# Second attention of a two-layer network on one core: where the value products stand in a step, where the layer matrices are made, and when the last slots are told

## The chip, the core and the metric

The kernel runs on one core of one Trainium2 chip. The core has five engines that the text names as the profile does: PE (matrix products and transposes; PEld are the weight loads that go with them), DVE (vector), ACT (scalar functions and copies), POOL (vector work and indirect DMAs) and SP (DMA issue). They run their own instruction streams and wait for each other on semaphores. Products land in PSUM, which has 8 banks of 128 x 512 float32 numbers. The metric is the device time of one launch in microseconds, as the median of several runs.

## What is computed

The input is 32 sequences of 128 tokens with 128 features, `x`, and one condition vector for each sequence. The network has two layers, each a chain of a conditioned map, an attention, a second conditioned map and a feed-forward part. Everything is in float32. The change lies in the second layer, which is, cut to what matters:

```python
# experts: a gate picks 2 of 4 experts for each sequence, plus a shared one
y = sum_e w[e] * (gelu(x @ ew1[e] + eb1[e]) @ ew2[e] + eb2[e]) + gelu(x @ sw1 + sb1) @ sw2 + sb2
# attention, 16 heads of 8
Q, K, V = relu(y @ Wq + bq), relu(y @ Wk + bk), relu(y @ Wv + bv)
scores = mask(Qh @ Kh.T / sqrt(8))            # key mask and causal mask
out = softmax(scores) * query_mask @ Vh + y
y = gamma * (out - mean) / sqrt(var + 1e-8) + beta
# a low-rank conditioned map: y = y + y @ M, with M of each sequence from its condition
# slots: 64 slots a sequence
alpha = softmax over the 8 largest of ((gelu([y, slot_mean] @ w1 + b1) @ w2 + b2) / tau)
si = (alpha.T @ y) / alpha.sum                # what each slot takes in
S_new = gru(si, slots)                        # r, z, n gates
T = softmax(q(S_new) @ k(S_new).T * scale) @ v(S_new) + S_new
out = alpha @ (layernorm(T) @ wvp + bvp) @ wo + bo
```

The output of the kernel is the stream with that last `out` added.

## The kernel before

**Tiling.** The stream X lies in SBUF with the features on the partitions; a chunk is 4 sequences, 512 columns, and there are 8 chunks. The first layer runs before the part that matters here. The second layer runs in a loop at the end (from L1479) of rounds `i`, in turns of TURN = 32 rounds, one turn for each of NP = 4 pairs of chunks, and two turns of rounds more for what trails. In a turn, with `r = i // 32` and `k = i % 32`:

- k = 0 to 23 are the **expert phase** of pair r: each round runs one `ins` and one `outs` piece (`shared_in`, `chosen_in`, `shared_out`, `chosen_out`, L860 to 913). A `chosen_in` multiplies X with an expert's fetched weights `ew` and ACT makes `he` (gelu) of it; a `chosen_out` multiplies `he` with `ew`.
- k = 23 and 24 to 31 each call `advance` with one of the pair's 8 sequences, and k = 0 to 2 of the next turn call it without one, to drain: the **attention**. In the last pair nothing of experts follows: that is the **tail**.

**An attention step.** `advance` (L1412) is a software pipeline written out by hand. Each call starts one sequence (masks and scores), works on the one before it (`w1`: highest, weights, early), on the one two before (`t1`: turned, kept, early_weights), three before (`v1`: values, valued), four before (`b1`: back, sums, normed) and five before (`n1`: moments). The functions are at L959 to 1072:

- `masks(hg)` and `scores()`: products into one PSUM bank for each of four head groups. 12 blocks of 128 rows of scores come of a sequence: `s_0` to 7 for the late queries and 8 to 11 for the early ones.
- `highest(hg)`: DVE takes maxima (`s1m`), each second one combines them (`s1max`); `weights(hg)`: ACT makes two exponentials (`s<-ps,s1max`); `early(hg)`: DVE subtracts the maxima for the early block and so frees the bank; `early_weights`: one exponential for all four (`s<-s`).
- `turned(c)`: PE transposes four blocks; `kept(c)`: ACT copies them to SBUF (`p1T`); `values`: 32 products with V; `valued`: ACT copies the sum (`oS`); `back`: PE transposes it; `sums`, `normed`: DVE divides (`rsum`, `o`), POOL adds to R.

PSUM banks have tags: scores take five banks A and B, all else three banks C in rotation (`ps()`, L294). In a step the order of takers is turned 1, turned 0, back, values, turned 2, so `values` takes the bank that `kept` 1 frees.

**What sets the order.** A scheduler orders the instructions of an engine by itself, except those that are pinned: ACT's activations always run in program order (`act`, L378), and so do DVE's and PE's while `pinned` isn't empty (L244 to 261), which `advance` sees to for its whole body. The rest is placed by a timetable: `plan` and `at` (L1339, L1391 to 1409) say in which round a generator starts, and `steps(i)` (L1465) moves each running generator one `yield` further a round. In attention rounds `steps` is called inside `advance`, as the last of `last`.

**The generators that the change touches.**

- `attention_inputs` (L915): V, the query mask, then q and k (a product, an activation, a product, an activation), then the mask sum (`tt` of 0.69 us), R, then the copies of V. For the first chunk of a pair it is in the timetable at k = 13; for the second one it is called by `next(inputs)` in k = 24 to 26.
- `after_attention` (L1110): moments, the root by ten small DVE instructions (`root_of`), `nmr`; then ACT normalizes R; transposes, X; products with the layer matrices, `xc`; transposes back, `xn`. For the second chunk it also starts `hs`.
- `layer_made` (L1095): a product on POOL (`rb`), four on PE, two additions on DVE: the two layer matrices `lw` of a pair. They lie in buffers `h1`, which the outputs `ot` of `slots_told` use too; `rb` lies in buffer `h3`, which the V of `attention_inputs` uses too.
- `hidden`, `routes_top`, `routes_exp`, `routes` (L1146 to 1207): gelu, logits and their 8 largest, two exponentials (`lg`), weights `al` and what the slots take in. `slots_new`, `slots_exp`: the gates and the slots' own scores.
- `slots_told` (L1266): the slots' softmax on DVE; transposes and copies (`sl_pT`, `y`); products with the values; moments and a root on DVE (`rsy`); transposes and copies (`ot`, `yT`); two more rounds of products and additions; a transfer of `ot` to the output. Five to six rounds long.

For pairs 0, 1 and 3 `slots_told` starts in rounds 5 and 7 of the turn after the slots' exponentials (L1407 to 1409), for pair 2 in rounds 26 and 27 of the turn itself, in the middle of pair 3's attention.

Of the kernel before, what the change touches and what calls it, by code (L numbers as in the profile page):

```python
# [19 lines left out]
P = 128  # L20
# [221 lines left out]
def program(ctx, tc, out, xT, packs, where):  # L242
# [37 lines left out]
    def w(name):  # L280
        pack, rows, c0, n = where[name]
        return loaded[pack][:rows, c0 : c0 + n]
# [21 lines left out]
    def mm(out_, lhsT, rhs, start=True, stop=True):  # L304
        T.matmul(out_, lhsT=lhsT, rhs=rhs, start=start, stop=stop)
# [72 lines left out]
    def act(*args, **kwargs):  # L378

        return tc.keep_in_program_order(A.activation(*args, **kwargs))  # L380
# [534 lines left out]
    def attention_inputs(g):  # L915
        xm = XMs[g]

        vf = mpool.tile([P, CB, D], F32, tag="h3", name="vf", bufs=1)
        qm = pool.tile([P, CB], F32, tag="qm", name="qm", bufs=2)
        for k in range(2):  # L920
            p = ps()
            p3 = p[:, : 2 * (D + 1)].rearrange("p (b d) -> p b d", d=D + 1)
            for e in range(2):
                mm(p3[:, e], xm[:, bass.ts(2 * k + e, S)], w("wv"))
            tt(V, vf[:, 2 * k : 2 * k + 2], p3[:, :, 0:D], outer(w("bv"), 2), ALU.add)
            V.tensor_scalar(qm[:, 2 * k : 2 * k + 2], p3[:, :, D], 0.0, None, ALU.not_equal)

        mask16 = pool.tile([P, CB, S], BF16, tag="mask16", name="mask16", bufs=2)
        G.tensor_scalar(mask16, inner(qm, S), -1.0, 1.0, ALU.mult, ALU.add)
        p = ps()  # L930
        mm(p, w("wq"), xm)
        qT = pool.tile([P, CH], F32, tag="qT", name="qT", bufs=2)
        act(qT, p, AF.Relu, bias=w("bq"))
        p = ps()
        mm(p, w("wk"), xm)
        kT = pool.tile([P, CH], F32, tag="kT", name="kT", bufs=2)
        act(kT, p, AF.Relu, bias=w("bk"))
        MVs[g] = pool.tile([P, CB, 2], F32, tag="mv", name="mv", bufs=2)
        prep[g] = qT, kT, mask16, qm
        yield  # L940

        p = ps()
        for b in range(CB):
            mm(p[:, bass.ts(b, S)], mask16[:, b, :], bars16)
        tt(V, mask16, b3(p), outer(causal, CB), ALU.add)
        yield

        p = ps()
        for b in range(CB):
            T.transpose(p[:, bass.ts(b, S)], xm[:, bass.ts(b, S)], ident)  # L950
        R = Rs[g] = pool.tile([P, CB, D], F32, tag="R", name="R", bufs=2)
        act(R, b3(p), AF.Copy)
        yield
        v, vo = V1[g % 2]
        for b in range(CB):
            act(v[:, 2 * b : 2 * b + 2, :, 0:8], vf[:, b].rearrange("p (h t d) -> p t h d", t=2, d=8), AF.Relu)
        nc.sync.dma_start(vo[64:P], v.rearrange("p (b t) h d -> p b t h d", t=2)[0:64, :, 1])
# [152 lines left out]
    def after_attention(g):  # L1110

        R, mv = Rs[g], MVs[g]
        for b in range(CB):
            moments(g, b)
        rs = root_of(mv[:, :, 1], "rs", 1e-8)
        nm = pool.tile([P, CB], F32, tag="nmr", name="nmr", bufs=2)
        V.scalar_tensor_tensor(nm, mv[:, :, 0], -1.0, rs, ALU.mult, ALU.mult)
        yield
        for b in range(CB):
            act(R[:, b, :], R[:, b, :], AF.Identity, scale=rs[:, b : b + 1], bias=nm[:, b : b + 1])  # L1120
        yield
        p = ps()
        for b in range(CB):
            T.transpose(p[:, bass.ts(b, S)], R[:, b, :], ident)
        V.scalar_tensor_tensor(col(g), p, w("gamma"), col(g), ALU.mult, ALU.add)
        yield
        p = ps()
        for b in range(CB):
            mm(p[:, bass.ts(b, S)], LWs[g][:, b, :], col(g)[:, bass.ts(b, S)])
        xc = XCs[g] = mpool.tile([P, CH], F32, tag="F", name="xc", bufs=3)  # L1130
        tt(V, xc, col(g), p, ALU.add)
        yield

        if g % 2:
            HSs[g // 2] = ps()
            for k in range(2):
                mm(HSs[g // 2][NS * k : NS * k + NS], w("f_w1a"), XCs[g - 1 + k])

        xn = XNs[g] = pool.tile([P, CB, D + 1], F32, tag="xn", name="xn", bufs=2)
        G.memset(xn[:, :, D : D + 1], 1.0)  # L1140
        p = ps()
        for b in range(CB):
            T.transpose(p[:, bass.ts(b, S)], xc[:, bass.ts(b, S)], ident)
        act(xn[:, :, 0:D], b3(p), AF.Copy)
# [121 lines left out]
    def slots_told(g):  # L1266
        s, m, sv = TKs[g]
        sn = SNs[g]
        V.tensor_reduce(m, s, AX.X, ALU.add)
        V.reciprocal(m, m)  # L1270
        tt(V, s, s, inner(m, NS), ALU.mult)
        yield
        p = ps()
        for q in range(2):
# [111 lines left out]
    for r in range(NP):  # L1386
        a, c = 2 * r, 2 * r + 1
        t = TURN * r
        if r:
            at(t + 13, attention_inputs, a)  # L1390
        at(t + 24, beta_added, a)  # L1391
        at(t + 24, beta_added, c)
        t += TURN
        at(t + 0, after_attention, a)
        at(t + 0, layer_made, r)
        at(t + 3, after_attention, c)
        at(t + 7, hidden, r)
        at(t + 8, routes_top, a)
        at(t + 9, routes_top, c)
        at(t + 12, routes_exp, r)  # L1400
        at(t + 13, routes, a)
        at(t + 14, routes, c)
        at(t + 17, slots_new, a)
        at(t + 18, slots_new, c)
        at(t + 25, slots_exp, r)

        t += 26 if r == NP - 2 else TURN + 5  # L1407
        at(t, slots_told, a)
        at(t + (1 if r == NP - 2 else 2), slots_told, c)
    line = []  # L1410

    def advance(item=None, between=()):  # L1412

        line.append(item)
        w1, t1, v1, b1, n1 = (line[-k] if k <= len(line) else None for k in (2, 3, 4, 5, 6))

        def do(it, name, *args):
            if it:  # L1420
                it[name](*args)

        first, last = between or ((), ())
        pinned.append(True)
        do(item, "masks", 0)
        do(w1, "highest", 0)
        do(w1, "highest", 1)
        if w1 or t1:
            do(v1, "kept", 2)
        do(t1, "turned", 1)  # L1430
        do(w1, "weights", 0)
        do(t1, "kept", 1)
        do(t1, "turned", 0)
        do(w1, "weights", 1)
        for f in first:
            f()
        do(w1, "highest", 2)
        do(w1, "highest", 3)
        do(b1, "back")
        do(w1, "weights", 2)  # L1440
        do(v1, "values")
        do(w1, "early", 0)
        do(n1, "moments")
        do(t1, "kept", 0)
        do(w1, "early", 1)
        do(b1, "sums")
        do(w1, "early", 2)
        do(w1, "weights", 3)
        for hg in range(1, 4):
            do(item, "masks", hg)  # L1450
        do(item, "scores")
        do(t1, "early_weights")
        do(b1, "normed")
        do(v1, "valued")
        for f in last:
            f()
        do(t1, "turned", 2)
        do(w1, "early", 3)
        if not item:
            do(w1, "early_weights")  # L1460
        if not w1:
            do(t1, "kept", 2)
        pinned.pop()
# [10 lines left out]
    for i in range(END + 2 * TURN):  # L1474
        r, k = i // TURN, i % TURN
        if i < 24:
            if i == 0:
                first_pieces()
            if i == 23:  # L1479
                advance(attention(0, 0))  # L1480
            continue
        if r < NP and k == 0:
            ins, outs, _ = (p + q for p, q in zip(experts(2 * r), experts(2 * r + 1)))
            ins[0]()
        if k < 3 and 1 <= r <= NP:
            advance()
        if k >= 24 and r < NP:
            b = k - 23
            if k == 24:
                inputs = attention_inputs(2 * r + 1)  # L1490
            between = [], [lambda: steps(i)]
            if k < 27:
                between[k > 25].append(lambda: next(inputs, None))
            if k == 25:
                between[1].append(lambda: next(inputs))
            advance(attention(2 * r + b // CB, b % CB) if b < 2 * CB else None, between)
            continue
        if r < NP:
            if k:
                ins[k]()  # L1500
            if k == 23:

                act(cst[0:1, 0:1], zeros[0:1, 0:1], AF.Exp)
            outs[k]()
            if k == 23:
                advance(attention(2 * r, 0))
        steps(i)
# [30 lines left out]
```

## Time and profile before

| what | us |
|---|---|
| median of 3 runs (lowest, highest) | 1293.98 (1291.41, 1294.65) |
| the profiled execution | 1292.62 |
| its span | 1290.8 |
| first layer and what is mixed with it, up to 748 | 748 |
| attention of turn 0, 1, 2, 3, first to last exponential | 63.0, 43.0, 43.1, 52.4 |
| expert phases, three, from first to last piece | 77 to 82 each |
| tail behind the last attention | 91.8 |

The mean granted clock of PE is 0.934. PE is busy 1122.5 us (87% of the span), PEld 716.1, DVE 752.3, ACT 741.9 and POOL 489.0. In a row of busy times by stretch, each engine has its microseconds and, in brackets, its instructions; then come the granted clock (1.00 is full), the share of the DMA engines and GB/s. In the chain of waits each line is a start, a length, an engine and what it worked on; the line that follows is what waited for it. In the timeline of an engine each line is a start, a length and the operation; a bracket at its end tells how long the engine was idle before it and who released it.

### The profile page before, as it was taken

What the parts mean: (1) busy time and instruction counts of PE and PEld (TensorE: products, weight loads), DVE (VectorE), ACT (ScalarE), POOL (GpSimd) and SP (SyncE); (2) the same over time, 40 slices, a digit from 0 to 9 for tenths busy, and PEclk for the clock granted to TensorE, in tenths of its full rate; (3) what the DMA queues carried; (4) which work ended last, traced back from release to release, by engine and by line L of the source; (5) the groups of instructions that cost most, each with busy time, mean ns of one, the idle gap of its engine ahead of it and who ended that gap; (6) DMA issues with size and microseconds to landing.
All of it is one profiled execution on the core that took longest, in us unless ns stands there. A gap on an engine that the chain in (4) does not pass through costs nothing. (4 is left out here: it accounts for less than half of the span.)

```text
span 1290.8 us, 24290 instructions
## 1 busy us (share of the span) xinstructions
PE 1122.5 (87%) x9509; PEld 716.1 (55%) x9509; DVE 752.3 (58%) x1996; ACT 741.9 (57%) x1857; POOL 489.0 (38%) x433
## 2 busy tenths in 40 slices
PE   4999899989999899898988677998999899987655
PEld 1555555445554455455545446676677667766433
DVE  1344748465684655836545467556755675568443
ACT  2666565665646646545355555676965596567421
POOL 1565555546555455534354531133222321312000
PEclk9999999989999989889898887999999999999765
DMA  6000000000000000000242210143024302400000
GB/s 258 1 1 2 1 1 1 1 1 1 1 2 1 1 1 1 1 1 1 93 129 64 81 36 6 56 146 104 11 77 136 109 10 76 134 21 11 18 0 17
DMA packets 18322, 51.99 MB, mean 40 GB/s; under 512 B 1568, under 2 KB 7840, under 8 KB 17952
## 3 DMA queue, kind: packets, MB, share of 16 engines
q0 software_dynamic: 9648, 40.01, 10.0%
q1 hardware_dynamic: 7984, 9.38, 2.3%
q8 instruction: 75, 1.23, 0.4%
q10 hardware_dynamic: 576, 1.05, 0.2%
q14 instruction: 39, 0.32, 0.1%
HBM read 46.25 MB, written 2.10 MB: 37 GB/s over the span
## 5 line engine op out<-in xcount | busy, mean ns | idle before, releaser
L380 ACT ACTIVATE s_sb<-ps,s_max 128x128 f32<-128x128 f32 x512 | 139.2, 383 | 132.6 <-DVE s_max L256 126.3
L256 POOL TENSOR_TENSOR s_sb<-s_sb,s_sum 128x1024 f32<-128x1024 f32 (+1 forms) x64 | 119.7, 1871 | 76.7 <-DVE s_sum L256 58.0
L256 PE MATMUL ps<-hT,w_attn 128*128 128x512 f32 x256 | 125.0, 618 | 10.9 <-DVE hT L256 10.9
L256 POOL TENSOR_TENSOR s_half<-s_sb 128x512 f32<-128x512 f32 x62 | 79.5, 1282 | 110.6 <-ACT s_sb L380 110.5
L256 POOL DMA_INDIRECT ew<-in_expert,rows x64 | 63.2, 987 | 124.4 <-DVE ye L256 98.2
L380 ACT ACTIVATE qk<-ps 128x512 f32<-128x512 f32 x128 | 74.4, 615 | 62.1 <-PE ps L256 61.6
L256 DVE TENSOR_REDUCE s_max<-ps 128x4 f32<-128x512 f32 x128 | 81.2, 674 | 49.0 <-PE ps L256 48.7
L380 ACT ACT_TABLE_LOAD x61 | 78.3, 1283 | 52.4 <-DVE s_max L256 38.9
L380 ACT ACTIVATE s<-ps,s1max 128x128 f32<-128x128 f32 x256 | 79.3, 400 | 39.5 <-DVE s1max L256 31.6
L256 DVE TENSOR_REDUCE s_sum<-s_half 128x8 f32<-128x256 f32 x62 | 25.8, 416 | 121.3 <-POOL s_half L256 121.2
L256 PEld LDWEIGHTS ps<-qk 64*128 64x128 f32 x1024 | 68.0, 195 | 37.4 <-issue 37.4
L256 PEld LDWEIGHTS ps<-hT,w_attn 128*128 128x128 f32 x256 | 47.5, 195 | 70.3 <-issue 48.4
L256 PE MATMUL ps<-he,ew 128*128 128x128 f32 x512 | 77.6, 291 | 5.8 <-ACT he L380 4.9
L380 ACT ACTIVATE he<-ps,ew 128x128 f32<-128x128 f32 x256 | 70.7, 377 | 20.2 <-issue 10.7
L256 PE MATMUL ps<-qk 64*128 64x128 f32 x1024 | 81.6, 294 | 0.0
L256 PEld LDWEIGHTS ps<-he,ew 128*128 128x128 f32 x512 | 67.8, 195 | 22.3 <-ACT he L380 11.6
L256 PE MATMUL ps<-w_base,s_sb 128*128 128x128 f32 x512 | 75.1, 291 | 3.6 <-ACT s_sb L380 2.7
L256 PE MATMUL ps<-pT,v 128*64 128x128 f32 x1024 | 73.2, 287 | 4.7 <-DVE X L256 2.5
L256 PE MATMUL ps<-X,ew 128*128 128x128 f32 x512 | 73.6, 278 | 0.7 <-DMA ew<-in_expert,rows 0.7
L256 DVE TENSOR_REDUCE s1m<-ps 128x6 f32<-128x384 f32 x128 | 65.0, 548 | 14.3 <-PE ps L256 14.3
L256 PEld LDWEIGHTS ps<-X,ew 128*128 128x128 f32 x512 | 65.6, 192 | 7.8 <-issue 6.1
L256 PEld LDWEIGHTS ps<-pT,v 128*64 128x64 f32 x1024 | 57.5, 142 | 17.5 <-issue 7.1
(298 smaller groups left out, 2429.4 us busy)
## 6 DMA issues: line engine op xcount, KB each, us to landing
v1o<-v SPq DMA_DIRECT2D x8, 256.0 KB, 3.0
out_x<-ot SPq DMA_DIRECT2D x8, 256.0 KB, 2.3
X<-in_xT ACTq DMA_DIRECT2D x4, 256.0 KB, 7.2
X<-in_xT SPq DMA_DIRECT2D x4, 256.0 KB, 9.8
w_attn<-in_attn POOLq DMA_DIRECT2D x1, 1024.0 KB
w_lowr<-in_lowr SPq DMA_DIRECT2D x1, 1024.0 KB
ew<-in_expert,rows POOLq DMA_INDIRECT x64, 5.3
w_ffn<-in_ffn SPq DMA_DIRECT2D x1, 928.0 KB, 10.4
```

Of the source, the lines that this page charges most:

```text
L256: ins = f(*args, **kwargs)
L380: return tc.keep_in_program_order(A.activation(*args, **kwargs))
```

## The change

- In `advance` the order of a step is new: the exponentials of two head groups come ahead of the copies of `kept` 2, those of the others ahead of `kept` 1 and `kept` 0; the last two maxima come ahead of what `first` holds; `values` stands behind the scores.
- `attention_inputs` yields between the products and the activations of q and k, so it has one round more, and the calls for the second chunk move accordingly.
- The moments and the root of `after_attention` and the softmax of `slots_told` are pinned to their places in program order.
- `layer_made` of pairs 1 to 3 starts in round 19 of the pair's expert phase and not at the start of the next turn.
- `slots_told` of pair 2 starts, as that of the others, in rounds 5 and 7 of the turn after, which is the tail.

```diff
--- before.py
+++ after.py
@@ -930,11 +930,12 @@
         p = ps()
         mm(p, w("wq"), xm)
         qT = pool.tile([P, CH], F32, tag="qT", name="qT", bufs=2)
+        pk = ps()
+        mm(pk, w("wk"), xm)
+        kT = pool.tile([P, CH], F32, tag="kT", name="kT", bufs=2)
+        yield
         act(qT, p, AF.Relu, bias=w("bq"))
-        p = ps()
-        mm(p, w("wk"), xm)
-        kT = pool.tile([P, CH], F32, tag="kT", name="kT", bufs=2)
-        act(kT, p, AF.Relu, bias=w("bk"))
+        act(kT, pk, AF.Relu, bias=w("bk"))
         MVs[g] = pool.tile([P, CB, 2], F32, tag="mv", name="mv", bufs=2)
         prep[g] = qT, kT, mask16, qm
         yield
@@ -1110,11 +1111,13 @@
     def after_attention(g):
 
         R, mv = Rs[g], MVs[g]
+        pinned.append(True)
         for b in range(CB):
             moments(g, b)
         rs = root_of(mv[:, :, 1], "rs", 1e-8)
         nm = pool.tile([P, CB], F32, tag="nmr", name="nmr", bufs=2)
         V.scalar_tensor_tensor(nm, mv[:, :, 0], -1.0, rs, ALU.mult, ALU.mult)
+        pinned.pop()
         yield
         for b in range(CB):
             act(R[:, b, :], R[:, b, :], AF.Identity, scale=rs[:, b : b + 1], bias=nm[:, b : b + 1])
@@ -1266,9 +1269,11 @@
     def slots_told(g):
         s, m, sv = TKs[g]
         sn = SNs[g]
+        pinned.append(True)
         V.tensor_reduce(m, s, AX.X, ALU.add)
         V.reciprocal(m, m)
         tt(V, s, s, inner(m, NS), ALU.mult)
+        pinned.pop()
         yield
         p = ps()
         for q in range(2):
@@ -1388,11 +1393,13 @@
         t = TURN * r
         if r:
             at(t + 13, attention_inputs, a)
+            at(t + 19, layer_made, r)
         at(t + 24, beta_added, a)
         at(t + 24, beta_added, c)
         t += TURN
         at(t + 0, after_attention, a)
-        at(t + 0, layer_made, r)
+        if not r:
+            at(t + 0, layer_made, r)
         at(t + 3, after_attention, c)
         at(t + 7, hidden, r)
         at(t + 8, routes_top, a)
@@ -1403,10 +1410,8 @@
         at(t + 17, slots_new, a)
         at(t + 18, slots_new, c)
         at(t + 25, slots_exp, r)
-
-        t += 26 if r == NP - 2 else TURN + 5
-        at(t, slots_told, a)
-        at(t + (1 if r == NP - 2 else 2), slots_told, c)
+        at(t + TURN + 5, slots_told, a)
+        at(t + TURN + 7, slots_told, c)
     line = []
 
     def advance(item=None, between=()):
@@ -1425,30 +1430,30 @@
         do(item, "masks", 0)
         do(w1, "highest", 0)
         do(w1, "highest", 1)
+        do(t1, "turned", 1)
+        do(w1, "weights", 0)
+        do(t1, "turned", 0)
+        do(w1, "weights", 1)
         if w1 or t1:
             do(v1, "kept", 2)
-        do(t1, "turned", 1)
-        do(w1, "weights", 0)
-        do(t1, "kept", 1)
-        do(t1, "turned", 0)
-        do(w1, "weights", 1)
+        do(w1, "highest", 2)
+        do(w1, "highest", 3)
         for f in first:
             f()
-        do(w1, "highest", 2)
-        do(w1, "highest", 3)
         do(b1, "back")
         do(w1, "weights", 2)
-        do(v1, "values")
         do(w1, "early", 0)
+        do(w1, "early", 1)
         do(n1, "moments")
-        do(t1, "kept", 0)
-        do(w1, "early", 1)
-        do(b1, "sums")
+        do(t1, "kept", 1)
         do(w1, "early", 2)
         do(w1, "weights", 3)
+        do(b1, "sums")
+        do(t1, "kept", 0)
         for hg in range(1, 4):
             do(item, "masks", hg)
         do(item, "scores")
+        do(v1, "values")
         do(t1, "early_weights")
         do(b1, "normed")
         do(v1, "valued")
@@ -1489,10 +1494,10 @@
             if k == 24:
                 inputs = attention_inputs(2 * r + 1)
             between = [], [lambda: steps(i)]
+            if k < 26:
+                between[0].append(lambda: next(inputs))
             if k < 27:
-                between[k > 25].append(lambda: next(inputs, None))
-            if k == 25:
-                between[1].append(lambda: next(inputs))
+                between[1].append(lambda: next(inputs, None))
             advance(attention(2 * r + b // CB, b % CB) if b < 2 * CB else None, between)
             continue
         if r < NP:
```

## The prediction

> **What bounds it now.** I read the busy time by stretches first, because the change touches three kinds of stretch: an attention of the second layer (the middle two of four are alike), an expert phase, and the tail.
>
> ```profile
> 1017.50:1060.70 43.20, 36.77 (x778) 27.40 (x777) 33.26 (x114) 36.79 (x107) 10.12 (x13) 0.96 0.06 18
> 1146.60:1199.00 52.40, 39.98 (x808) 30.56 (x807) 42.10 (x156) 38.97 (x112) 10.17 (x13) 0.94 0.03 7
> 932.00:1014.00 82.00, 80.18 (x644) 59.92 (x643) 46.43 (x177) 49.94 (x126) 21.32 (x24) 1.00 0.38 114
> 996.00:1002.00 6.00, 6.00 (x48) 5.81 (x47) 3.35 (x10) 3.79 (x13) 1.99 (x3) 1.00 0.85 276
> 1002.00:1008.00 6.00, 6.00 (x47) 4.50 (x46) 3.31 (x9) 3.38 (x12) 1.86 (x2) 1.00 0.78 214
> 1199.00:1291.00 92.00, 53.24 (x375) 35.54 (x374) 38.63 (x155) 22.78 (x47) 1.36 (x3) 0.65 0.04 12
> ```
>
> Columns: stretch, its length, busy time of PE, PEld, DVE, ACT, POOL, granted clock, DMA. In attention no engine is full (PE and ACT 85% each): a chain of waits decides. Pair 2's `slots_told` makes turn 3's attention 9.2 us longer than turn 2's, with 30 PE and 42 DVE instructions more. The experts are bound by PE (80.2 of 82.0). In the tail everything idles: latency alone counts. The chain of waits in a steady attention step:
>
> ```profile
> 920.56 1.03 DVE s1m L256 x2
> ...
> 921.62 0.30 DVE s1max L256
> ...
> 922.00 0.63 ACT s L380 x2
> 922.63 0.49 ACT p1T L380
> ...
> 923.17 2.66 PE ps L256 x100
> ```
>
> From 920.56 to the next `s1m` at 925.85 is one step, about 5.28 us. The maxima release the first exponentials; the copy behind them, `kept` 1, frees the PSUM bank that `values` takes; PE then does values, masks and scores in one run, and the scores release the next maxima. The tail, on ACT:
>
> ```profile
> 1206.57 1.64 ACT L380 ACTIVATE R<-R,nmr,rs 128x128 f32<-128x128 f32 x4
> 1220.19 0.60 ACT L380 ACTIVATE xn<-ps 128x512 f32<-128x512 f32 x1 [11.99 <-PE ps L256]
> 1223.35 1.65 ACT L380 ACTIVATE R<-R,nmr,rs 128x128 f32<-128x128 f32 x4 [2.56 <-DVE nmr L256]
> 1231.67 0.60 ACT L380 ACTIVATE xn<-ps 128x512 f32<-128x512 f32 x1 [6.67 <-PE ps L256]
> ...
> 1234.27 1.28 ACT L380 ACT_TABLE_LOAD   x1
> 1240.03 0.42 ACT L380 ACTIVATE lg<-lg 128x256 f32<-128x256 f32 x1 [4.47 <-DVE lg L256]
> ```
>
> The 11.99 us ahead of `xn` hold a wait for the layer matrices: their buffers are freed only by pair 2's output transfer, 2.33 us. The load of the exponential's table at 1234.27 is hidden under the wait for `lg`.
>
> **Slots of pair 2, part one: out of the attention.** 52.40 − 43.20 = −9.2; I take −9.3 by the exponentials (1146.67 to 1199.07 against 1017.59 to 1060.67).
>
> **Part two: into the tail.** I count from Z, the last exponential of attention (1199.07). Before, `R` of the first chunk ran at Z+7.5, `xc` at Z+19.3, `hs` at Z+34.5, and the routes' weights `al` were ready at Z+44.4 and Z+45.6. After: the matrices have long been made, so R at Z+6.7, X 2.2 later, `xc` 2.9 after that (Z+11.8); the second chunk's root, behind it, puts its R at Z+15.7, X at 17.9, `xc` at 20.8 and hs at Z+25.8, 8.7 earlier. Then it turns. Pair 2's slots start in tail rounds 5 and 7, so their normalizing, value products and root interleave on DVE with the routes' logits, and ACT's program order puts the routes' exponentials (round 12) behind the second `yT`. Some 3.5 us of slot work on DVE delays the second `lg` to Z+38; the root and the additions give y at Z+42, yT ends at about Z+45. Only then comes the table load, now with nothing to hide it. The trace has the load at 1.28 us with the next instruction 0.01 us behind (1232.27, 1.28, then `hs` at 1233.57). The Trainium skill (ScalarE: Activation LUTs, What ACT_TABLE_LOAD costs) adds a drain of about 1380 ns to each such switch, about 2.66 us in all; by the row exponentials start at Z+46.3, by the page at Z+47.7. I take the row. The second `al` comes at about Z+51.5 against Z+45.6: +5.8. Everything after it is the old chain. The output transfers of pair 2 fall here too; on SP nothing stands behind them but the last outputs, 0. Slots in sum: −3.5 (tail between +2 and +10: the lower end if DVE's slot work finds gaps, the upper at this clock, 0.65).
>
> **The steps of attention.** `values` goes behind the scores, so the bank it waits for leaves the chain. What is late next: masks of the fourth head group need the bank freed by `early` 2, and that waits for the exponentials of group 2 and DVE's order; from the step's start I make it 3.6 to 3.9 us, scores at 4.3, so only 0.1 us is gained. Against it: the output copy `oS` stands last in ACT's order and waits for values, which now start when the scores end. In the tail `values` 1200.92 led to `oS` 1202.22, so 1.30 us. With values issued 0.07 before the next maxima's start, oS begins 1.23 into the next step and ends at 1.71, where the first exponentials, behind it in ACT's order, could have begun at 1.44: +0.27. Net +0.17 for each of 4 plain steps, +0.7; the step with the `v` copies (four of 0.20 ahead of the exponentials) +0.9; the drain, where `kept` 2 moves into the chain and oS waits too, 3.96 becomes 4.9: +0.9. The first steps gain: q and k activations leave their place between exponentials (−0.2), the mask addition of 0.69 and the slots' softmax leave their place ahead of the maxima (−0.7), another −0.2: −1.1. Sum +1.4 a turn, four turns, +5.6. Bounds: −8.6 (below) and +10, if oS's delay also holds up `back` each step.
>
> **R of the second chunk.** In DVE's new order its root is fixed behind `xc` of the first; before, it ran between X and xc.
>
> ```profile
> 948.88 0.60 ACT L380 ACTIVATE xn<-ps 128x512 f32<-128x512 f32 x1 [0.70 <-PE ps L256]
> 949.38 1.64 ACT L380 ACTIVATE R<-R,nmr,rs 128x128 f32<-128x128 f32 x4
> 950.92 2.15 ACT L380 ACTIVATE he<-ps,ew 128x128 f32<-128x128 f32 x8
> ```
>
> `nmr` was ready at 947.89; a root of 2.55 us behind xc and b7's moments puts it near 950.9. So R goes to 951.0 and the experts' `he`, queued behind it on ACT, 1.6 us later; PE has 0.3 to 1.1 us of other work and then waits for he. PE is full from 950 to 1008, so what it loses isn't made up: 1.2 for each of three turns, +3.6 (0 to 1.7 each).
>
> **Layer matrices.** For turns 1 to 3, four products (1.13 us at 939.58) and two additions (0.69 each) move from the drain to the expert phase's rounds 19 and 20; POOL's product of 1.03 goes between two weight fetches, which are issued ahead of use, 0. In the drain PE idled around them (the next hidden product waited for ACT until 941.00), so nothing comes back. In their new place PE's rows read 6.00 of 6.00. Here the Trainium skill (Perfetto Trace Analysis, Identifying the Most-Contended Engine) speaks against me: pipelined matmuls make PE's busy time a bad measure, and weight loads are the better one. By those rows, 5.81 and 4.50 of 6, the second has 25% free and the cost would be 0; by PE's, 1.13. Whole-phase PE of 80.2 in 82.0 with 644 products says the stream itself is the limit. I take 0.9 a turn, +2.7 (0 to 3.4).
>
> **Sum.** −3.5 + 5.6 + 3.6 + 2.7 = +8.4 on the profiled execution's 1292.6: 1301.0. The median of the runs shown is 1.4 above that execution; I leave it inside the range.
>
> **Rivals.** A, the other side: the bank of `values` was the true limit. Then without it the step falls to ACT's own busy time, 4.74 us, −0.54 in 16 plain steps = −8.6 in place of the +2.8 I put on those: 1301.0 − 11.4 = 1289.6, and 1284 if R and the matrices hide in PE too. For it: the chain names exactly that copy ahead of PE's run; against it: the second path by `early` 2 is only 0.1 shorter, and `oS` must follow values. It decides where scores start before 3.8 us of a step. B: PE's phase does have room (the weight-load view), R and matrices cost nothing: 1292.6 − 3.5 + 5.6 = 1294.7, the same within measurement. For it: PEld 59.92 of 82. C: tail worse, the table switch costs 2.66 and slot work runs at the low clock on DVE and PE in series: +5 to 7, 1307. Against it: the low clock touches PE alone, whose parts here are short.
>
> **How the numbers follow.** A measurement tells about 0.3%, 3.9 us, from no change. My sum or near it 0.47, C 0.17, B 0.19, A 0.17. Faster (under 1290.1) 0.15, same 0.21, slower (over 1297.9) 0.64. The range: 1288 takes in A's plain case, 1308 C; beyond lie about 0.2.
>
> **What would show it.** Turn 3's attention at about 44 us between first and last exponential, like the others; plain steps of 5.3 to 5.5 in the chain with `oS` in it; ACT idle ahead of `s` released by PE. R of the second chunk near Z+13 in turns 1 to 3, PE waiting for `he` behind it; expert phases 82 to 84 us. In the tail `hs` near Z+26, a table load directly ahead of `lg`, `al` past Z+50. Steps under 5.1 would make the forecast wrong, as would expert phases no longer than before.

## The result and the profile after

The changed kernel takes 1303.08 us, the median of 5 runs (1299.24 to 1307.43), beside 1293.7 for the kernel before (5 runs): a ratio of 1.0078, 95% interval 1.0052 to 1.0104, so +10 us. The forecast was 1301.0, +8.4 by its sum. The profiled execution of the changed kernel is the fastest of its five: 1299.24 us, span 1297.4. Its span is 6.6 us longer than that of the kernel before, so some 3 us of the loss can't be placed by it.

The busy times by stretch, cut where the same stretches of the kernel lie now (an attention of turn 2, one of turn 3, the expert phase between turns 1 and 2, the tail):

```profile
1026.20:1071.20 45.00, 37.75 (x788) 29.07 (x787) 33.06 (x104) 37.25 (x106) 9.65 (x13) 0.96 0.07 20
1159.40:1203.50 44.10, 35.65 (x779) 27.97 (x779) 33.13 (x104) 36.93 (x106) 9.49 (x13) 0.96 0.04 9
938.70:1022.60 83.90, 79.90 (x635) 58.91 (x634) 48.91 (x192) 48.36 (x124) 21.77 (x25) 1.00 0.38 113
1203.50:1297.40 93.90, 59.03 (x404) 39.84 (x402) 46.29 (x206) 24.97 (x53) 1.37 (x3) 0.62 0.04 12
```

Turn 3's attention is as short as turn 2's: the slots have left it. Each attention is longer than 43.2, the expert phase is 1.9 us longer with no more PE busy time in it, and the tail is 2.1 longer. A steady attention step in the chain of waits:

```profile
917.06 0.50 ACT p1T L380
917.56 0.04 issue
917.60 3.21 PE ps L256 x106
920.81 0.02 issue
920.83 0.61 ACT oS L380
921.44 1.14 ACT s L380 x4
922.58 0.50 ACT p1T L380
923.08 0.04 issue
923.12 3.21 PE ps L256 x106
```

DVE's maxima have left the chain and `oS` has come in: 5.52 us from one PE run to the next. PE's run of 3.21 us is `back`, masks, scores and values; it ends with values, `oS` waits for that, four exponentials wait on ACT behind oS, then `kept` 2, and that frees the bank which `back`, first on PE, takes. The tail on ACT:

```profile
1209.76 1.64 ACT L380 ACTIVATE R<-R,nmr,rs 128x128 f32<-128x128 f32 x4
1216.23 0.60 ACT L380 ACTIVATE xn<-ps 128x512 f32<-128x512 f32 x1 [4.83 <-PE ps L256]
1218.12 1.65 ACT L380 ACTIVATE R<-R,nmr,rs 128x128 f32<-128x128 f32 x4 [1.29 <-DVE nmr L256]
...
1244.41 0.56 ACT L380 ACTIVATE yT<-ps,w_base 128x256 f32<-128x256 f32 x1
1244.99 1.28 ACT L380 ACT_TABLE_LOAD   x1
1246.29 0.72 ACT L380 ACTIVATE lg<-lg 128x256 f32<-128x256 f32 x2
```

The wait for the matrices is gone (4.83 idle ahead of `xn`, not 11.99), and the exponentials `lg` stand behind the second `yT` and a table load that nothing hides.

To set kernels side by side I use one measure: the starts of the `early_weights` exponentials (`s<-s`), eight in an attention. Their distances are the steps. "Gap" is from a turn's last one to the next turn's first, "tail" from the last one of all to the end of the span.

| us | before | after |
|---|---|---|
| first one of turn 0 | 763.04 | 761.01 |
| attention, turns 0, 1, 2, 3 | 47.53, 33.87, 33.90, 43.23 | 52.61, 35.86, 35.81, 34.97 |
| gaps | 86.68, 95.65, 95.17 | 88.37, 97.54, 97.39 |
| plain step; step with the V copies | 5.28; 5.22 | 5.52; 6.19 |
| tail | 91.73 | 93.84 |

### The profile page after: what moved, and what is told of

It reads as the page before. It is cut to its first block, busy times and chain, and to the rows that moved or that the text cites. A ratio compares the mean times of both kernels' runs of the same rounds, so it can differ in the third digit from the quotient of the medians.

```text
span 1297.4 us, 24330 instructions
## 1 busy us (share of the span) xinstructions
PE 1129.1 (87%) x9509; PEld 719.5 (55%) x9509; DVE 752.8 (58%) x1996; ACT 741.6 (57%) x1857; POOL 490.1 (38%) x433
## 3 DMA queue, kind: packets, MB, share of 16 engines
q8 instruction: 75, 1.23, 0.4%
## 5 line engine op out<-in xcount | busy, mean ns | idle before, releaser
L256 DVE TENSOR_REDUCE s_sum<-s_half 128x8 f32<-128x256 f32 x62 | 25.8, 415 | 122.5 <-POOL s_half L256 122.4
L256 PEld LDWEIGHTS ps<-hT,w_attn 128*128 128x128 f32 x256 | 47.5, 195 | 70.3 <-issue 48.1
L256 PEld LDWEIGHTS ps<-w_base,s_sb 128*128 128x128 f32 x512 | 58.5, 148 | 15.3 <-issue 4.0
```

What stands on the lines that cost most here:

```text
L256: ins = f(*args, **kwargs)
```

## The experiments: one part at a time

My theory, S: the order of the step pays most of the loss, since `oS` now waits for values and stands ahead of the exponentials; the slots gain. Its rivals: B, that the boundary between attention and experts pays (pins and matrices), and, inside the step, K, that `kept` 2 and the bank it frees hold `back`.

**Only the step order** (with the extra round of `attention_inputs`): the part of the diff in `advance`, `attention_inputs` and the loop, put into the kernel before.

> Only the new order of the attention step, with the extra round of attention_inputs that goes with it. Theory S (the steps and the ramp pay most of the loss): plain steps of 5.5 us in place of 5.28, the time from a turn's last exponential to the first of the next as before or 1 to 2 us longer, in all +6 to +11 us. Theory B (the boundary pays: the pinned root and the moved matrices cost the 1.7 to 1.9 us between the attentions): +3 us or less.

Ratio 1.0125 (1.0109 to 1.0141), +16 us: more than S gave. Plain steps are 5.52, the step with V copies 6.19; the four attentions grow by 5.4, 3.1, 3.7 and 3.1 us, the gaps by 1.2 us at most and 1.2 in sum. The spans of the two profiled executions differ by 15.4 us, so here nearly all of the price is placed. B falls: the boundary is not needed for the loss.

**Only the slots of pair 2.**

```diff
-        t += 26 if r == NP - 2 else TURN + 5
-        at(t, slots_told, a)
-        at(t + (1 if r == NP - 2 else 2), slots_told, c)
+        at(t + TURN + 5, slots_told, a)
+        at(t + TURN + 7, slots_told, c)
```

> Only pair 2's slots told in the tail. By the terms of the forecast -9.3 + 5.8 = -3.5 us. By the traces of before and after, which show a tail only 2.1 us longer, -6 to -8 us. If the gain in turn 3's attention was due to something else, 0 or above.

Ratio 0.9946 (0.9929 to 0.9962), −7.0 us. Turn 3's attention goes from 43.23 to 34.42 us, −8.8; the tail from 91.7 to 95.0, but the second `al` is transposed only 0.8 us later behind the last exponential (Z+50.2, before Z+49.4). The other 2.5 of the tail's 3.3 us came behind it, where PE has the same 114 products in both kernels, at a granted clock of 0.54 against 0.62.

**Only the layer matrices of two pairs.** Moved alone for pair 3 too, they would hold both `h1` buffers that pair 2's outputs need in turn 3's attention, so that part of the change needs the slots' move.

```diff
+            if r < 3:
+                at(t + 19, layer_made, r)
-        at(t + 0, layer_made, r)
+        if r in (0, 3):
+            at(t + 0, layer_made, r)
```

> Only the layer matrices of pairs 1 and 2 made in round 19 of their expert phases; pair 3's stay at the turn's start, since they and pair 2's outputs in turn 3's attention need the same two buffers. By the terms of the forecast (PE is full there, nothing comes back in the drain) +0.9 each, +1.8 us. If the drain's PE time does come back, or PE has room in the experts, -2 to 0 us.

Ratio 1.0036 (1.0024 to 1.0048), +4.7 us. The first two gaps grow by 1.7 and 1.0 us. The third, which loses pair 2's products and gets none, is 1.1 us shorter, and the first step behind it 1.5: in the drain something seems to come back. The tail, whose code is the same, is 4.2 us longer (clock 0.61 against 0.65), so the ratio overstates this part.

**Only the pins** on `after_attention` and `slots_told`.

> Only the pins on the root of after_attention and on the slots' softmax. By the terms of the forecast R of the second chunk comes 1.6 us later and stops the experts' PE for 1.2 us in each of three turns: +3.6 us. By the trace of the changed kernel, where PE waited 0.18 us for that R: 0 to +1 us.

Ratio 1.0017 (1.0010 to 1.0024), +2.2 us. Gap and attention together grow by 0.1 us in each of turns 1 to 3 (0.03, 0.10 and 0.14; turn 1's gap is 1.3 longer, its attention 1.3 shorter); the tail, in which the pins stand too, is 1.6 longer at a clock of 0.63. Of this 1.1 lies behind the second `al`, at 0.58 against 0.62. The ratio is between the two expectations.

**Slots and matrices of all three turns together.**

```diff
+            at(t + 19, layer_made, r)
...
-        at(t + 0, layer_made, r)
+        if not r:
+            at(t + 0, layer_made, r)
...
+        at(t + TURN + 5, slots_told, a)
+        at(t + TURN + 7, slots_told, c)
```

> Pair 2's slots in the tail and the layer matrices of all three turns made in the experts; nothing else. Against the run with the slots alone (-7 us): by the forecast's term +2.7 us; by the gaps between attentions in the run of two matrices (+1.7 and +1.0 us) +4 us for three; if PE hides them, 0.

Ratio 0.9959 (0.9945 to 0.9973), −5.3 us, so the matrices cost about 1.7 beside the slots (by the two intervals, uncertain by some 2.5 us). Against the run with the slots alone the gaps are 1.15, 0.65 and 0.83 us longer, and the tail 0.9 shorter.

**The changed kernel with the old step order.**

> The changed kernel with the step order and the attention_inputs of before: slots, matrices and pins stay. If the parts add up: -7.0 + 3 to 4 + 2.2 = -1 to -2 us on the kernel before, and the new order is then worth +11 to +12 us in the changed kernel. If the new order and the rest interact (the run of the order alone gave +16), the sum is off by some 5 us: near +3 us or near -6 us.

Ratio 0.9960 (0.9946 to 0.9974), −5.2 us: the sum is off, as in the last case of the expectation, but not because the order interacts. The new order is worth +10.1 − (−5.2) = +15.3 in this company, as alone (+16.2). What is smaller here than the expectation had it are the matrices (+1.7) and the pins (+0.1, uncertain by some 2.5 us).

## The experiments: inside the step

**Values behind the scores and nothing else**, in the kernel before.

```diff
-        do(v1, "values")
         do(w1, "early", 0)
...
         do(item, "scores")
+        do(v1, "values")
```

> The kernel before with values behind the scores and nothing else moved. Theory S: kept 2 and the first exponentials wait on ACT behind an oS that comes 1.3 us after the scores: plain steps 5.4 to 5.8 us, +4 to +10 us. Rival A of the forecast (the bank that values takes was the limit): steps 4.75 to 5.0 us, -5 to -9 us.

Ratio 1.0098 (1.0083 to 1.0114), +12.7 us, the plain step 5.95 us, both more than S gave. This is rival A of the forecast put to the test, and it fails. The chain, of this kernel:

```profile
919.27 1.03 DVE s1m L256 x2
920.30 0.02 issue
920.33 0.29 DVE s1max L256
920.62 0.94 DVE s1m L256 x2
921.56 0.61 ACT s L380 x2
922.16 0.49 ACT p1T L380
922.65 0.52 ACT s L380 x2
```

The first maxima are combined by 920.62 (920.33 and 0.29), but their exponentials start 0.92 us later, since on ACT they stand behind `oS` and `kept` 2 (the chain names the second pair of maxima, which belong to the other head groups and end at the same moment):

```profile
920.50 0.60 ACT L380 ACTIVATE oS<-ps 128x512 f32<-128x512 f32 x1 [1.25 <-PE ps L256]
921.05 0.60 ACT L380 ACTIVATE p1T<-ps 128x512 f32<-128x512 f32 x1
921.54 0.62 ACT L380 ACTIVATE s<-ps,s1max 128x128 f32<-128x128 f32 x2
```

ACT idles for 1.25 us until values are done, and the exponentials and all behind them are late. Exponentials ahead of copies (the other half of the new order) win back 0.43 of the 0.67 us.

**Values back in their place, exponentials still ahead of the copies**, in the changed kernel.

```diff
         do(w1, "weights", 2)
+        do(v1, "values")
...
         do(item, "scores")
-        do(v1, "values")
```

> The changed kernel with values back ahead of the masks, the exponentials still ahead of the copies. Theory S: values then waits for the later kept 1 and holds the masks and scores, steps of 6.0 us or more, +8 us or more on the changed kernel: the two halves of the new order need each other. If values behind the scores is what costs, steps go to 5.2 us and the kernel gains 5 us or more.

Ratio 1.0175 (1.0148 to 1.0203), +23 us on the kernel before, +13 on the changed one; plain steps 6.82 us. So in the plain step each half of the order alone (5.95 and 6.82) is worse than both together (5.52), and both together are worse than neither (5.28). Over the whole kernel values alone cost less than the whole order, 12.7 beside 16.2: the order has its price in turn 0 besides.

**Kept 2 first again**, in the changed kernel.

```diff
+        if w1 or t1:
+            do(v1, "kept", 2)
         do(t1, "turned", 1)
...
         do(w1, "weights", 1)
-        if w1 or t1:
-            do(v1, "kept", 2)
```

> The changed kernel with kept 2 back ahead of the exponentials. Theory S (the output copy waits for values behind the scores, and early 2 sets the scores): kept 2 now pushes the exponentials, plain steps 5.5 to 6.0 us, +0 to +8 us on the changed kernel. Theory K (back waits for the bank that kept 2 frees, and holds masks and scores behind it on PE): steps fall to 5.3 us or less, -4 us.

Ratio 1.0010 (1.0001 to 1.0019), +1.3 us on the kernel before, some 9 less than the changed kernel: a miss for S in size and for K in place. Plain steps are 5.55 us, as S had it: K's bank alone isn't what bounds them. The gain is elsewhere: turn 0's attention takes 47.89 us and not 52.61. (The first step of the other turns is 4.9 and not 5.7, but the gaps ahead are 0.3 to 0.6 longer.) Turn 0 has maxima that come late. ACT of the kernel before, and PE's `back`, in turn 0:

```profile
778.43 0.60 ACT L380 ACTIVATE p1T<-ps 128x512 f32<-128x512 f32 x1 [0.59 <-PE ps L256]
783.04 0.62 ACT L380 ACTIVATE s<-ps,s1max 128x128 f32<-128x128 f32 x2 [4.01 <-DVE s1max L256]
783.85 1.06 PE L256 MATMUL ps<-w_base,oS 128*128 128x128 f32 x4
```

And of the changed kernel:

```profile
782.41 1.14 ACT L380 ACTIVATE s<-ps,s1max 128x128 f32<-128x128 f32 x4 [4.23 <-DVE s1max L256]
783.43 0.61 ACT L380 ACTIVATE p1T<-ps 128x512 f32<-128x512 f32 x1
784.09 1.11 PE L256 MATMUL ps<-w_base,oS 128*128 128x128 f32 x4 [1.66 <-ACT p1T L380]
```

Before, the copy ran as soon as PE had turned its blocks, 4 us ahead of the exponentials; now it sits behind exponentials that wait for DVE, and with it `back`, for which PE idles 1.66 us, and all that PE has behind `back`. The other runs agree: turn 0's attention takes 53.0 us with the order alone and 54.0 with values back and the exponentials ahead, but 49.0 with values behind the scores alone, beside 47.5 in the kernel before. How much of the 9 us this is stays open: the spans of the two profiled executions differ by 2.8 us only, since here turn 0 began 2.4 us later and the profiled execution of the changed kernel was 3.8 below its median.

**oS behind the first two exponentials of the next step**, in the changed kernel.

```diff
         do(w1, "weights", 0)
+        do(b1, "valued")
...
-        do(v1, "valued")
```

> The changed kernel with the output copy oS moved behind the first two exponentials of the next step. Theory S, if oS alone bounds: exponentials start 0.46 us earlier, plain steps 5.05 to 5.15 us, -8 us on the changed kernel. If the way by early 2 is as late, 5.4 to 5.5 us and -1 to -2 us.

Ratio 1.0086 (1.0058 to 1.0114), no faster than the changed kernel: both expectations missed. Plain steps are 6.00 us. The exponentials do not start earlier: they come 1.83 us behind the start of the maxima (924.21), as in the changed kernel (921.44 behind 919.61).

```profile
925.30 0.66 PE L256 MATMUL ps<-w_base,s 128*128 128x128 f32 x4
926.04 0.62 ACT L380 ACTIVATE s<-ps,s1max 128x128 f32<-128x128 f32 x2 [1.37 <-DVE s1m L256]
927.21 0.66 PE L256 MATMUL ps<-w_base,s 128*128 128x128 f32 x4 [0.64 <-ACT oS L380]
928.21 0.66 PE L256 MATMUL ps<-w_base,oS 128*128 128x128 f32 x4 [0.35 <-ACT p1T L380]
928.70 0.67 PE L256 MATMUL ps<-mask,twice 128*128 128x256 bf16 x6
929.30 0.91 PE L256 MATMUL ps<-km,qT 32*64 32x256 f32 x32
```

Their own maxima were combined by 925.56 (`s1max`); the maxima in the bracket belong to other head groups and end only at 926.03. What ended just ahead, at 925.96, is the last transpose of `turned` 2, which in the new order stands behind values on PE. It reads the older of the two buffers `s`, the one that these exponentials write, and ACT's wait on PE ended at 926.00. In the changed kernel `turned` 2 ends at 921.36 and oS at 921.43: the two are tied, and taking oS away gains nothing. What the move costs is that oS now stands ahead of `kept` 2 and pushes it: `back` comes 2.17 us behind the first exponentials in place of 1.68, and the masks and scores behind it.

So a later oS doesn't help either. In the changed kernel several waits are nearly tied: `back` for `kept` 2, the exponentials for `oS` and for `turned` 2, both behind values; taking one away shows the next.

**A better tail.** Slots in the tail as above, and the last pair's routes two rounds earlier.

```diff
-        at(t + 12, routes_exp, r)
-        at(t + 13, routes, a)
...
+        u = t - 2 if r == NP - 1 else t
+        at(u + 12, routes_exp, r)
+        at(u + 13, routes, a)
```

(and `slots_new` likewise)

> The kernel before with pair 2's slots told in the tail, and in the tail the routes' exponentials and what follows two rounds earlier, so that they stand ahead of the second yT on ACT. By the forecast's account of the tail (the exponentials wait behind yT, and the table load lies open): alpha 5 to 6 us earlier than in the run with the slots alone moved, -12 us on the kernel before. If DVE's slot work, not ACT's order, holds the logits: -7 to -8 us as there.

Ratio 0.9883 (0.9862 to 0.9905), −15 us, more than expected; the tail falls from 95.0 to 84.5. ACT's order, not DVE's slot work, had held the exponentials:

```profile
1219.58 0.56 ACT L380 ACTIVATE yT<-ps,w_base 128x256 f32<-128x256 f32 x1
1220.16 1.28 ACT L380 ACT_TABLE_LOAD   x1
1221.45 0.42 ACT L380 ACTIVATE lg<-lg 128x256 f32<-128x256 f32 x1
1222.70 0.42 ACT L380 ACTIVATE lg<-lg 128x256 f32<-128x256 f32 x1 [0.83 <-DVE lg L256]
1229.01 0.60 ACT L380 ACTIVATE ot<-ps 128x512 f32<-128x512 f32 x1 [5.89 <-PE ps L256]
```

`lg` starts at Z+30.7, where Z is 1190.73, the last exponential of attention; with the slots alone moved it was Z+41.8. Nothing hides the table load here either, but the second yT, 7 us later, no longer stands ahead of it. The second `al` is transposed 7.1 us earlier (Z+43.2 for Z+50.2). Up to there the granted clock is 0.76 and not 0.63, behind it 0.63 and not 0.54, so the clock has a share in the 10.5 us, and no run parts it from the order's.

**And the bank, the other way.** The same with `kept` 1 ahead of the first exponentials, values staying ahead of the masks.

```diff
-        do(w1, "weights", 0)
         do(t1, "kept", 1)
+        do(w1, "weights", 0)
```

> The kernel before with pair 2's slots in the tail and the tail's routes two rounds earlier (that alone gave -15 us), and in the step kept 1 ahead of the first exponentials, values staying ahead of the masks. It asks for what the change was to remove, the wait of values for that bank, without the later oS. Turned 1 ends some 1.1 us after the maxima start, so kept 1 costs the first exponentials about 0.2 us and lets values and the scores come 0.3 us earlier: plain steps 4.9 to 5.1 us in place of 5.28, -20 us on the kernel before. If early 2 is already as late: 5.2 to 5.4 us, -13 to -16 us.

Ratio 0.9838 (0.9818 to 0.9858): 1273.48 us, −21 us, the fastest of all and better than both kernels. Plain steps are 5.08 us. The four attentions together take 144.1 us, 5.3 less than in the run ahead of it (149.4), which agrees with the 0.45% between the two ratios; by the spans of the two profiled executions only 1.4 of it is left, since turn 0 began 2.2 us later and its gap was 1.5 longer there, and why is open.

```profile
917.85 1.27 ACT L380 ACTIVATE p1T<-ps 128x512 f32<-128x512 f32 x2 [0.26 <-PE ps L256]
919.02 1.65 ACT L380 ACTIVATE s<-ps,s1max 128x128 f32<-128x128 f32 x6
```

Two copies run where ACT had waited for the maxima, and six exponentials follow without a break. Counted from the start of the maxima (917.13 here, 920.56 before), the exponentials come 0.45 us later (1.89 for 1.44), but values come 0.51 earlier (2.10 for 2.61). The wait for the bank of values was worth 0.2 us a step; it is taken away by an earlier copy, not by later values.

## Why the forecast came out right, and where it was wrong

The sign, the total and the direction of every part were right. The size of the total was luck: the step order came out 9.7 us dearer than forecast, the other three parts together 8.0 us cheaper. (In company means with the other parts of the change in.)

| part | forecast | measured |
|---|---|---|
| slots of pair 2 | −3.5 | −7.0 (−9.2 to −4.9), alone |
| step order | +5.6 | +16.2 (14.1 to 18.2) alone; +15.3 in company |
| R of the second chunk (pins) | +3.6 | +2.2 (1.3 to 3.1) alone; +0.1 in company |
| layer matrices | +2.7 | +1.7, beside the slots |
| sum | +8.4 | +10 |

- **Slots out of attention**, −9.3: measured −8.8.
- **Slots in the tail**, +5.8: mis-sized. `hs` came at Z+25.3 as forecast (25.8), and the table load of 1.28, which nothing hides, with `lg` 0.02 behind it as the row of before had it; the drain of about 1380 ns that the Trainium skill (ScalarE: Activation LUTs, What ACT_TABLE_LOAD costs) adds doesn't show. What I overrated was the slot chain between: the second yT ended at Z+41.4 and not Z+45, the second `al` started at Z+47.7 (before Z+45.6) and not Z+51.5, and the whole tail is 2.1 us longer, with the slots alone 3.3. Why the slot chain was faster isn't worked out. The cause that I named, ACT's program order, is borne out by the run with the routes two rounds earlier.
- **Plain steps**, +0.17 each by an `oS` that is 0.27 late: +0.24, with oS 1.22 us into the step where I had 1.23. But oS isn't the only cause: `turned` 2, which I left out, frees the buffer of the exponentials as late. I had named `early` 2 as the next wait; the chain has `kept` 2 and `back` there. Kept 2 ahead again left the steps at 5.55, with PE's masks waiting for `early`, so the two are as good as tied.
- **Step with V copies** +0.9: measured +0.96. **Ramp** −1.1: the first step of turns 1 to 3 changed by −0.8, −0.6 and +0.4 against the kernel with the old order (5.66, 5.84 and 5.67 against 6.44, 6.44 and 5.24). **Drain** +0.9: the last step grew by 0.9, 0.7 and 0.0. The attentions of turns 1 to 3 grow by 2.1, 2.0 and 2.4 us over the kernel with the old order, where I had +1.4.
- **Step order, the term that failed**: +1.4 a turn. With the order alone turn 0's attention grew by 5.4 us, and each later turn, attention and gap ahead of it, by 2.8 to 4.3; beside the other parts it was 5.7 in turn 0 (which began 2.8 us earlier) and 1.7 to 2.7 later. I gave turn 0 the same as the others, though it has late maxima and a chain of its own. What I had not costed is that a copy moved behind exponentials also moves behind whatever those wait for. In the later turns the step with the V copies and the plain steps came as forecast or up to 0.2 dearer; the ramp's gain came only in part. Of the +15.3 in company the spans show 9.4. The moved maxima and the extra round of `attention_inputs` go with the order in every run that has it, so their own share is not shown.
- **R of the second chunk**: it came 1.0 to 1.2 us later behind the first R where I had 1.6, and PE did lose about the 1.2 that I had. Before, the four transposes of R lay between products of the experts; now PE has none of these left (the kernel before, then the changed one):

```profile
949.91 0.33 PE L256 MATMUL ps<-w_base,R 128*128 128x128 f32 x1
950.08 0.39 PE L256 MATMUL ps<-X,ew 128*128 128x128 f32 x2
950.30 0.32 PE L256 MATMUL ps<-w_base,R 128*128 128x128 f32 x1
```

```profile
955.03 2.40 PE L256 MATMUL ps<-X,ew 128*128 128x128 f32 x20
957.60 1.48 PE L256 MATMUL ps<-w_base,R 128*128 128x128 f32 x4 [0.18 <-ACT R L380]
```

The wait ahead of them is 0.18 us, but they then follow ACT's R one by one, four in 1.48 us, where four transposes of a step take 0.66: about 1.0 in all. In the gaps of the kernel with the old order the pins cost 0.9 to 1.0 each. What failed is that nothing would be made up: the attentions of that kernel are 2.1 us shorter in sum than in the run of slots and matrices, 1.6 of it in one, and over the kernel the pins came to +0.1. Why attention gives it back is open. (Among the signs I put R near Z+13; by my own sum of 951.0 it is Z+20 there, and it came at Z+19.2.)
- **Layer matrices**: 1.15, 0.65 and 0.83 us in the gaps against 0.9 forecast. This agrees with PE's full row and not with the 25% free in the rows of the weight loads, which the Trainium skill (Perfetto Trace Analysis, Identifying the Most-Contended Engine) prefers as a measure. It isn't sure to better than the gap itself: in the last run above the first gap grew by 1.5 with no matrices moved. I had that nothing comes back in the drain; the gaps that also lose products grow less than the first, and the 0.9 us that the tail gained was left out.
- **Rival A** is refuted in its form (values behind the scores: +12.7, not −8.6), though its premise was half right: the bank of values does cost 0.2 us a step of the 0.54 that A had. **B** was nearly right on R (+0.1 in company), not on the matrices, and its total was 8 us too low. **C** did not come: the tail is not as long.
- **Signs**: `hs`, the table load ahead of `lg` and the expert phase of 83.9 us came as I had them, the plain steps at 5.52 just above my 5.3 to 5.5; `al` past Z+50 did not come.

## What to carry over

In a step where two engines feed each other, an instruction that is moved later on one queue delays all that stands behind its reader on the other: ask of each moved copy what waits behind it, in the steady step and in the steps whose inputs come late, and of each moved product what stands behind it on its own queue (here the transposes that free a buffer). To shorten a wait for a bank, release the bank earlier, in the idle time that the queue already has, before making its taker later. Work told into an idle tail is cheap only as long as no in-order queue puts it ahead of the tail's own chain: here two rounds in a timetable came with 8 us, a part of it perhaps the clock's.

## What was not expected of the hardware

Tails with the same code differ by up to 4 us between profiled executions (91.73 in the kernel before, 95.89 with two pairs' matrices moved), at granted clocks of 0.65 and 0.61, while plain attention steps of the same order agree within 0.02 us from kernel to kernel. The stretch behind the second `al` shows it best, since there PE has the same 114 products in every kernel:

| granted clock | us | kernels |
|---|---|---|
| 0.63 | 41.3 | the two with the routes two rounds earlier |
| 0.62 | 42.3; 42.7 | before; changed |
| 0.58 | 43.0; 43.4 | order alone; pins alone |
| 0.54 | 44.8; 44.9 | slots alone; two pairs' matrices |

ACT's normalizing of R doesn't follow this clock: four take 1.64 to 1.65 us in the tail and in the expert phase at 1.00. Why the clock is lower in one execution than in another no run shows. A tail's length from one profile is no measure of a change of 2 us.
